# Padding rows scattered by index, a sum by matmul, and 48 steps of attention moved from the ordering of the entries to the experts

## The chip, the cores and the metric

The kernel runs on one core of one Trainium2 chip. The metric is device time in microseconds, as the median of several runs. One execution of it was taken by the hardware profiler; its trace gives the start and duration of every instruction. The engines are called as the profile calls them: PE (TensorE matmuls) and PEld (its weight loads), DVE (VectorE), ACT (ScalarE), POOL (GpSimd) and SP (SyncE, which here only issues DMAs). Each engine works through its own queue in order.

## The reference, cut to what matters

For x of 8 batches of 1024 rows of 256 numbers the kernel computes x + s * g.

```
xn = layernorm(x)
# attention over the 4 heads of each row, not over rows
q, k, v = (xn @ W + b).reshape(b, s, 4, 256)      for Wq, Wk, Wv
scores  = (q*cos . k*cos + q*sin . k*sin) / 16     # 4 x 4 for each row
s = softmax(scores) @ v, heads to rows (swapaxes), @ Wo + bo
# mixture of 8 experts, each row takes the best 2
gates = sinkhorn(xn @ router_w.T + router_b, 3 rounds)   # sums over experts, then over rows
top 2 gates of each row, normalised to sum 1
expert_out = sum over the 2: gate * ((relu(xn @ wg) * (xn @ wp)) @ wo)
g = silu(xn + expert_out)
out = x + s * g
```

## The kernel before, in words

The 8192 rows are 64 tiles of 128 rows, in 16 blocks of four. The work runs in five stages; two of them share TensorE with attention.

**Preparation.** `prepare` (L371 to L424) normalises a block, stores it row by row in `xn_d` (L422, in HBM) and turned in `xT_d` (L418). `xn_d`, and the result of the experts `z_d`, have 256 rows more than there are tokens: padding rows, where padded entries may point. After the last store GpSimd issues two plain DMAs: zeros into the padding rows of `xn_d` (L1032) and a padding list over all of `list_d` (L1035, 9088 KB).

**Routing and ordering.** `route` (L454) runs the gates, with one maximum and three sums over partitions on GpSimd (`partition_all_reduce`, L494 and L505). `order` (L540) finds for each of the 16384 entries (a row and its gate) its place in a list sorted by expert; it sums counts over partitions once more on GpSimd (L579). Beside both, `setup_values` prepares weights.

**Scattering the entries.** `scatter` (L635) writes the entries into `list_d` by index: 16 groups of 8 indirect DMAs, each of one column of 128 entries. The places of a group are cast to integers on VectorE (`place`, L639), and that cast is held behind `newest["dot"]`, the newest dot product that attention has issued when the group is written down. So the groups are spread over attention's steps: the first group comes ahead, then 32 steps, then each group followed by 15 steps, then 13. Ahead of it SP copies all of `xn_d` into `z_d` (L1060): the experts add their results to it.

**Attention** is a generator (`attention`, L819), which issues one small step at each call. A tile's scores (`score`, L653) are 9 steps: four chunks of matmuls into `py` (L662) that ScalarE copies to `qk` (L669), one step of four dot products on VectorE (`junk`, L675), and four in which the keys are weighted (`kx`, L700) and dotted. So a tile has 16 dots. `soften` (L713) is two steps for each block. `value` (L726) of a tile comes a block later, between the scores: two halves of matmuls `pu` (L745) with `u` (L752), then the mix of the heads. Ahead of the experts the mix is four matmuls with a `mixer` (L777), 3 steps in all; beside the experts, VectorE weights `u` itself (16 instructions, L764 and L768) and the matmul is a narrow one (L772), 4 steps in all. So a block is 50 steps ahead of the experts and 54 beside them, and the first block, which has no older values, 38. 32 + 15 times 15 + 13 = 270 steps are issued before the experts.

**Experts.** The list is cut in 71 tiles of 256 entries, each of one expert; 68 always run. For each, `fetch_expert` reads the entries (L840), casts the rows (L850), gathers them from `xn_d` (`xg`, L853, indirect), and loads three weight matrices (L864). `expert` turns the rows on TensorE (`ptr_g`, L878), multiplies (`pg`, `pp`, L890; ScalarE and VectorE between), and `down` (`po`, L906) scales by the gate and adds into `z_d` by index (L919). After each of the 408 steps of the experts one step of attention is issued, after every fourth two: 510 steps. The last three tiles run only if needed (L1075).

**Tail.** For each block, `fetch_last` (L947) loads z, x and s on SP, `finish` (L962) computes silu(z) * s + x and stores it (L967, GpSimd). Six steps of attention stand ahead of each, until attention is done; a block's result needs attention's result of its whole batch.

The order on each engine is that of the compiled program: the framework's scheduler takes instructions in nearly the order of the source and moves some ahead by estimated times. Names with a number in the program (`py_0_2881`) are one tile's buffers.

Of the kernel before, what the change touches and what calls it, by code (L numbers as in the profile page):

```python
# [9 lines left out]
F32 = mybir.dt.float32  # L10
# [6 lines left out]
P = 128  # L17
# [13 lines left out]
def recurrent_kernel(  # L31
# [20 lines left out]
    nc = tc.nc  # L52
    B, S, D = x.shape
    H = phase.shape[0]
    E, _, FF = ffn_g.shape
# [3 lines left out]
    R = HD // D  # L59
# [8 lines left out]
    M = G // P  # L68
# [35 lines left out]
    n = 1  # L104
# [349 lines left out]
    def route(pool, hot, entries):  # L454
# [22 lines left out]
        def flat(a):  # L477
            return a.rearrange("p b e -> p (b e)")
# [20 lines left out]
        for turn in range(SINKHORN_ITERS):  # L499
            if turn:  # L500
                nc.vector.tensor_reduce(rs, share, AX.X, ALU.add)
                nc.vector.reciprocal(rs, rs)
                nc.vector.tensor_tensor(share, share, per_tile(rs), ALU.mult)
            nc.vector.tensor_reduce(cm, by_expert(share), AX.X, ALU.add)
            nc.gpsimd.partition_all_reduce(flat(cs), flat(cm), P, bass_isa.ReduceOp.add)  # L505
            yield
            nc.vector.reciprocal(cs, cs)
            nc.vector.tensor_tensor(by_batch(share), by_batch(share), per_expert(cs), ALU.mult)
            yield
# [30 lines left out]
    def order(pool, hot, keep, placed):  # L540
# [35 lines left out]
        for i in range(R):  # L576
            rows = slice(i * J, (i + 1) * J)
            nc.vector.tensor_copy(quarter[rows, i], count[rows, :E])
        nc.gpsimd.partition_all_reduce(  # L579
            sums.rearrange("p i e -> p (i e)"),  # L580
            quarter.rearrange("p i e -> p (i e)"),
            P,
            bass_isa.ReduceOp.add,
        )
        total, prior = pool.tile([P, E], F32, name="o_total"), pool.tile([P, E], F32, name="o_prior")
        nc.vector.tensor_reduce(total, sums.rearrange("p i e -> p e i"), AX.X, ALU.add)
        nc.vector.tensor_tensor(
# [382 lines left out]
    def run(gen, n=None):  # L970
        done = 0
        while (n is None or done < n) and next(gen, StopIteration) is not StopIteration:
            done += 1
# [2 lines left out]
    xT_tiles, newest, attended, stored, beside_experts = {}, {}, set(), [], [False]  # L976
    x_rows, out_rows = (a.rearrange("b s d -> (b s) d") for a in (x, out))
    att_gen = attention()
    blank = const.tile([P, M * D], F32, name="blank")
    nc.vector.memset(blank, 0.0)  # L980
    empty = const.tile([P, M, LE], F32, name="empty")
    nc.vector.memset(empty, 0.0)
    for m in range(M):
        nc.vector.tensor_scalar(
            empty[:, m, :1], partition[:, :1], float(M), float(B * S + m), ALU.mult, ALU.add
        )

    ids = const.tile([P, T], F32, name="ids")
    nc.vector.tensor_copy(ids[:, :TB], column[:, :TB])
    n = TB  # L990
# [19 lines left out]
    with tc.tile_pool(name="prep", bufs=2) as prep:  # L1010
        with tc.tile_pool(name="setup", bufs=1) as setup:
            small_rows = fetch_setup(setup)
            for blk in range(7):
                fetch_rows(blk, prep, "x", 7)

            for blk, tag in ((7, "kx"), (8, "kx"), (9, "s_out"), (10, "s_out")):
                fetch_rows(blk, att, tag, 2)
            fetch_rows(11, att, "w", 1)
            bvT = setup_scores(setup, *small_rows)
            prepare(0, prep)  # L1020
        with tc.tile_pool(name="tail", bufs=1) as tail:
            for blk in range(12, T // TB):
                fetch_rows(blk, tail, f"x{blk}", 1)
            for blk in range(1, 4):
                prepare(blk, prep)
            linear(0, prep)
            for blk in range(4, T // TB):
                prepare(blk, prep)
                if blk % 4 == 3:
                    linear(blk - 3, prep)  # L1030
        with tc.issue_after(stored[-1].ins):
            nc.gpsimd.dma_start(  # L1032
                xn_d[B * S :].rearrange("(p m) d -> p (m d)", m=M), blank
            )
            nc.gpsimd.dma_start(  # L1035
                list_d.rearrange("(n p m) c -> p n (m c)", p=P, m=M),
                empty.rearrange("p m c -> p (m c)").unsqueeze(1).to_broadcast([P, N, M * LE]),
            )
    with tc.tile_pool(name="routing", bufs=1) as routing:
        hot = routing.tile([P, E, K, T], F32, name="hot")  # L1040
        entries = routing.tile([P, K * T * 2 + LE], F32, name="entries")
        nc.vector.memset(entries, 0.0)
        for n in range(K):
            nc.vector.tensor_copy(pairs_of(entries)[:, n, :, 0], ids)

        keep = routing.tile([P, E, K * T], F32, name="keep")
        nc.vector.memset(keep, 1.0)
        nc.vector.memset(keep[:, :, :1], 0.0)

        values = setup_values(bvT)  # L1050
        for n, _ in enumerate(route(routing, hot, entries)):
            if n > 2:
                run(values, 1)
        placed = []
        run(order(routing, hot, keep, placed))
        run(values)
        put = scatter(entries, placed[0])
        next(put)

        nc.sync.dma_start(z_d, xn_d)  # L1060
        run(att_gen, 32)
        for _ in put:
            run(att_gen, 15)
        run(att_gen, 13)
    before_experts = newest["score"]
    fin = ctx.enter_context(tc.tile_pool(name="fin", bufs=2))
# [2 lines left out]
    ffn = middle.enter_context(tc.tile_pool(name="ffn", bufs=2))  # L1069
    beside_experts[0] = True  # L1070
    for n, _ in enumerate(experts(0, SURE)):
        run(att_gen, 1 if n % 4 else 2)

    held = nc.values_load(first_spare[:1, :1], min_val=0, max_val=E)
    with tc.If(held < E):  # L1075
# [47 lines left out]
```

## Time and profile before

| what | value |
|---|---|
| median of 14 runs | 1714.77 us (1711.72 to 1716.53) |
| the profiled execution: its own time | 1714.96 us |
| its span, first to last instruction | 1713.2 us |
| mean granted TensorE clock | 0.976 |
| busy: PE, DVE, ACT, POOL | 1623.8, 1205.4, 432.5, 674.7 us |
| HBM read, written | 178.17, 76.41 MB |
| first matmul of an expert (`pg`) | 410.25 us |
| last matmul of the 68th expert (`po`) ends about | 1587.3 us |
| dots of a tile of the first block | about 10 us |
| a tile of attention ahead of the experts | about 12 us |

A line of a timeline has the start in us, the duration in us (of several instructions of one kind in a row, if there is an x and a number), the engine, the line of the kernel, the operation, what it writes and reads, the shapes, and in brackets how long the engine stood idle before it and what released it. A line of busy time by stages has the stretch, its length, and for PE, PEld, DVE, ACT and POOL the busy us and the number of instructions; then the granted clock of TensorE, the mean busy share of the 16 DMA engines and GB/s. A matmul in 32-bit floats leaves two records in the trace: eight matmuls of a tile's scores are 16 records of L662. Ends of matmuls are modelled, so records in a row overlap a little; what a run of them takes is read from the chain of waits, where only the time to the next is counted.

### The profile page before, as it was taken

How to read it: one execution, taken by the hardware profiler on the slowest of the kernel's cores; microseconds unless marked ns; L12 is line 12 of the kernel's file. 1: busy time of each engine (PE TensorE's matmuls, PEld its weight loads, DVE VectorE, ACT ScalarE, POOL GpSimd, SP SyncE). 2: the span in 40 equal slices, each digit the busy share in tenths (PEclk: the TensorE clock that was granted, in tenths of full speed). 3: DMA queues.
4: the chain of work that ended last, by engine and by line, in shares of the span. 5: the costliest groups of instructions: out<-in, count | busy, mean ns of one | idle time of the engine just before them, and what ended most of it. 6: DMA issues, size and time to landing. Idle time of an engine off the chain costs nothing.

```text
span 1713.2 us, 22964 instructions
## 1 busy us (share of the span) xinstructions
PE 1623.8 (95%) x7695; PEld 1002.8 (59%) x7695; DVE 1205.4 (70%) x3717; ACT 432.5 (25%) x816; POOL 674.7 (39%) x593
## 2 busy tenths in 40 slices
PE   6897799999999999999999999999999999999773
PEld 5373344445666666766666666666666666666331
DVE  6669999998575575765765756656657567476694
ACT  3742222222222212222222222222222222222322
POOL 0315876575243433343343434344423443331111
PEclk8898999999999999999999999999999999999887
DMA  8992022125544554544544544544545545542688
GB/s 271 360 358 89 31 73 62 58 66 199 148 120 127 141 130 114 149 119 111 164 119 113 147 124 119 152 115 132 145 111 141 140 117 129 141 109 52 214 262 305
DMA packets 149305, 247.48 MB, mean 144 GB/s; under 512 B 15304, under 2 KB 93168, under 8 KB 149008
## 3 DMA queue, kind: packets, MB, share of 16 engines
q1 hardware_dynamic: 105904, 164.42, 29.2%
q0 software_dynamic: 41264, 77.37, 19.6%
q10 hardware_dynamic: 2016, 4.20, 0.7%
q8 instruction: 62, 1.02, 0.2%
q14 instruction: 59, 0.48, 0.1%
HBM read 178.17 MB, written 76.41 MB: 149 GB/s over the span
## 4 chain that ended last, share of the span: by engine, by line
PE 78%; DVE 12%; DMA 6%; issue 2%; POOL 1%; ACT 1%; SPq 0%; POOLq 0%; ACTq 0%; DVEq 0%
PE py L662 18%; PE pg L890 14%; PE po L906 14%; PE pp L890 14%; PE pu L745 10%; DVE junk L675 5%; DVE kx L700 3%; PE ptr_g L878 2%; PE po_s L772 1%; DMA fz<-z_d 1%; PE ptr_x L410 1%; PE po_s L777 1%; DMA fs<-s_d 1%; DMA out_dram<-fz 1%; DMA z_d<-y,row 1%
## 5 line engine op out<-in xcount | busy, mean ns | idle before, releaser
L662 PE MATMUL py<-w_qk,xTa 128*128 128x512 f32 x1024 | 476.8, 601 | 27.0 <-ACT qk L669 27.0
L919 POOL DMA_INDIRECT z_d<-y,row x136 | 234.6, 1725 | 566.0 <-ACT y L916 473.1
L675 DVE CUSTOM_DVE_ANT_0 junk<-qk,kx,lg 128x256 f32<-128x256 f32 x768 | 323.6, 477 | 0.1
L662 PEld LDWEIGHTS py<-w_qk,xTa 128*128 128x128 f32 x1024 | 189.8, 191 | 222.1 <-issue 182.2
L675 DVE CUSTOM_DVE_ANT_0 junk<-qk,lg 128x256 f32<-128x256 f32 x256 | 113.2, 479 | 265.1 <-ACT qk L669 264.9
L669 ACT COPY qk<-py 128x512 f32<-128x512 f32 x256 | 149.6, 586 | 464.6 <-PE py L662 426.3
L890 PE MATMUL pg<-xgT,wg 128*128 128x256 f32 x1088 | 266.0, 386 | 0.3
L890 PE MATMUL pp<-xgT,wp 128*128 128x256 f32 x1088 | 259.0, 380 | 0.0
L906 PE MATMUL po<-wd,hid 128*128 128x256 f32 x1088 | 257.1, 382 | 0.0
L890 PEld LDWEIGHTS pg<-xgT,wg 128*128 128x128 f32 x1088 | 200.9, 190 | 89.2 <-issue 37.0
L745 PE MATMUL pu<-w_vo,xTa 128*32 128x512 f32 x2048 | 248.0, 597 | 0.3 <-PEq L1075 0.3
L906 PEld LDWEIGHTS po<-wd,hid 128*128 128x128 f32 x1088 | 203.3, 190 | 66.9 <-issue 43.3
L700 DVE TENSOR_TENSOR kx<-qk,mixrow 128x1024 f32<-128x1024 f32 (+1 forms) x256 | 233.5, 949 | 0.1
L890 PEld LDWEIGHTS pp<-xgT,wp 128*128 128x128 f32 x1088 | 205.5, 190 | 32.3 <-issue 3.3
L642 POOL DMA_INDIRECT list_d<-entries,place x128 | 179.7, 1404 | 76.0 <-DVE place L639 40.6
L899 DVE TENSOR_TENSOR hid<-pp,hid 128x512 f32<-128x512 f32 x136 | 93.3, 686 | 145.5 <-PE pp L890 145.5
L764 DVE SCALAR_TENSOR_TENSOR w<-u,sc,w 128x256 f32<-128x256 f32 x456 | 192.3, 477 | 0.9
L853 POOL DMA_INDIRECT xg<-xn_d,row x136 | 160.4, 1179 | 51.1 <-issue 47.8
L898 ACT ACTIVATE hid<-pg 128x512 f32<-128x512 f32 x136 | 81.2, 597 | 301.6 <-PE pg L890 286.8
L745 PEld LDWEIGHTS pu<-w_vo,xTa 128*32 128x32 f32 x2048 | 57.1, 109 | 132.1 <-issue 121.9
L916 ACT ACTIVATE y<-po,entry 128x256 f32<-128x256 f32 x136 | 57.1, 471 | 231.9 <-PE po L906 231.9
L752 DVE TENSOR_TENSOR u<-pu,b_vo 128x512 f32<-128x512 f32 x128 | 85.9, 682 | 17.7 <-PE pu L745 17.1
(208 smaller groups left out, 985.6 us busy)
## 6 DMA issues: line engine op xcount, KB each, us to landing
wg<-in_L_ffn_wg_dram SPq DMA_DIRECT2D x68, 512.0 KB, 3.8
wp<-in_L_ffn_wp_dram SPq DMA_DIRECT2D x68, 512.0 KB, 4.4
wd<-in_L_ffn_wo_dram SPq DMA_DIRECT2D x68, 512.0 KB, 3.9
list_d<-empty POOLq DMA_DIRECT2D x1, 9088.0 KB, 56.0
z_d<-xn_d SPq DMA_DIRECT2D x1, 8448.0 KB
x<-in_L_attn_x_dram SPq DMA_DIRECT2D x16, 512.0 KB, 8.4
xn_d<-x POOLq DMA_DIRECT2D x16, 512.0 KB, 5.7
s_d<-s_out SPq DMA_DIRECT2D x64, 128.0 KB, 3.3
```

The costliest lines, as they stand in the source:

```text
L642: put = nc.gpsimd.indirect_dma_start(list_d, bass.IndirectOffsetOnAxis(ap=piece[:, c : c + 1], axis=0), entries[:, at * 2 : at * 2 + LE], ...
L662: newest["score"] = nc.tensor.matmul(py, xT[:, t, k], w[:, k, cols], start=(k == 0), stop=(k == KD - 1),)
L669: nc.scalar.copy(flat[:, cols], py)
L675: newest["dot"] = nc.vector.tensor_tensor_reduce(junk, qk[:, 0, h], k, 1.0 / math.sqrt(D), lg[:, tile_no, E + at : E + at + 1], ALU.mult, ...
L700: nc.vector.tensor_tensor(kx[:, :w], k, mixrow[:, at : at + w].unsqueeze(2).to_broadcast([P, w, 2, D]), ALU.mult,)
L745: nc.tensor.matmul(pu[i * J : (i + 1) * J, :], xT[:, t, k, i * J : (i + 1) * J], w_vo[:, k, i, cols], start=(k == 0), stop=(k == KD - 1),)
L764: nc.vector.scalar_tensor_tensor(w[:, h], part, share, w[:, h], ALU.mult, ALU.add)
L853: nc.gpsimd.indirect_dma_start(xg[:, m], None, xn_d, bass.IndirectOffsetOnAxis(ap=row[:, m : m + 1], axis=0),)
L890: nc.tensor.matmul(dst[:, f], w[:, k, at : at + P], xgT[:, k], start=(k == 0), stop=(k == KD - 1),)
L899: nc.vector.tensor_tensor(h, pp, h, ALU.mult)
L906: nc.tensor.matmul(po[:, m], hid[:, f, m * P : (m + 1) * P], wd[:, f], start=(f == 0), stop=(f == KF - 1),)
L919: nc.gpsimd.indirect_dma_start(z_d, bass.IndirectOffsetOnAxis(ap=row[:, m : m + 1], axis=0), y[:, m], None, compute_op=ALU.add,)
```

## The change

The source is changed at five places. Line numbers in the text are those of the kernel before; behind the edits they are larger by 2 to 17.

- The padding rows of `xn_d` are no longer written by a plain DMA after the preparation. Two indirect DMAs on GpSimd, with the row numbers in a new tile `padding`, scatter a zero tile there, held behind the last sum over partitions of `route` (`newest["columns"]`). The zero tile `blank` is half as wide.
- `z_d` gets the rows of `xn_d` without the padding (still on SP, written down earlier in the source), and its padding rows from the zero tile by a DMA of their own. The scattered padding and this copy are declared not to depend on each other.
- The sum over partitions in `order` is a matmul of a 128 x 128 tile of ones with the counts, into PSUM, and a copy by VectorE, and no longer an operation of GpSimd.
- Ahead of the experts: 14 steps after the first group and 13 after each other one, and 13 at the end: 222 steps, and not 270.
- Beside the experts: two steps of attention after two of every five steps of the experts, and not after one of four: 572 steps, and not 510.

```diff
@@ route
-            nc.gpsimd.partition_all_reduce(flat(cs), flat(cm), P, bass_isa.ReduceOp.add)
+            newest["columns"] = nc.gpsimd.partition_all_reduce(
+                flat(cs), flat(cm), P, bass_isa.ReduceOp.add
+            )
@@ order
-        nc.gpsimd.partition_all_reduce(
-            sums.rearrange("p i e -> p (i e)"),
-            quarter.rearrange("p i e -> p (i e)"),
-            P,
-            bass_isa.ReduceOp.add,
-        )
+
+        pq = ps_gp.tile([P, R * E], F32, tag="gp", name="pq")
+        nc.tensor.matmul(
+            pq, ones, quarter.rearrange("p i e -> p (i e)"), start=True, stop=True
+        )
+        nc.vector.tensor_copy(sums.rearrange("p i e -> p (i e)"), pq)
@@ main part
-    blank = const.tile([P, M * D], F32, name="blank")
+    blank = const.tile([P, D], F32, name="blank")
...
+    padding = const.tile([P, M], mybir.dt.int32, name="padding")
+    nc.vector.tensor_copy(padding, empty[:, :, 0])
...
         with tc.issue_after(stored[-1].ins):
             nc.gpsimd.dma_start(
-                xn_d[B * S :].rearrange("(p m) d -> p (m d)", m=M), blank
-            )
-            nc.gpsimd.dma_start(
                 list_d.rearrange("(n p m) c -> p n (m c)", p=P, m=M),
...
+    copied = nc.sync.dma_start(z_d[: B * S], xn_d[: B * S])
+    tc.add_to_no_dep_group("padding", copied.ins)
+    nc.sync.dma_start(
+        z_d[B * S :].rearrange("(p m) d -> p m d", m=M),
+        blank.unsqueeze(1).to_broadcast([P, M, D]),
+    )
...
+        with tc.issue_after(newest["columns"].ins):
+            for m in range(M):
+                pad = nc.gpsimd.indirect_dma_start(
+                    xn_d,
+                    bass.IndirectOffsetOnAxis(ap=padding[:, m : m + 1], axis=0),
+                    blank,
+                    None,
+                )
+                tc.declare_no_dep(pad.ins, group="padding", reason="rows behind those copied")
+                tc.add_to_no_dep_group("padding", pad.ins)
         placed = []
         run(order(routing, hot, keep, placed))
         run(values)
         put = scatter(entries, placed[0])
         next(put)
-
-        nc.sync.dma_start(z_d, xn_d)
-        run(att_gen, 32)
+        run(att_gen, 14)
         for _ in put:
-            run(att_gen, 15)
+            run(att_gen, 13)
         run(att_gen, 13)
...
     for n, _ in enumerate(experts(0, SURE)):
-        run(att_gen, 1 if n % 4 else 2)
+        run(att_gen, 2 if n % 5 < 2 else 1)
```

## The prediction

> **What bounds the kernel now.** I read the busy tenths, then the busy time by stages, then the queues of TensorE, GpSimd and VectorE where the experts begin, then the tail.
>
> ```profile
> PE   6897799999999999999999999999999999999773
> ```
>
> One digit is 42.8 us. TensorE is full but for the ends and slices 4 and 5 (128 to 214 us). By stages (PE, PEld, DVE, ACT, POOL busy, granted clock, DMA share, GB/s):
>
> ```profile
> 197.00:280.00 83.00, 82.65 (x382) 35.26 (x381) 83.00 (x282) 17.54 (x33) 60.48 (x55) 1.00 0.20 63
> 600.00:1000.00 400.00, 399.88 (x1917) 266.48 (x1916) 255.84 (x757) 94.09 (x183) 155.70 (x139) 1.00 0.50 129
> ```
>
> From 197 us up to the experts TensorE and VectorE are both full; beside the experts TensorE alone is (399.88 of 400), VectorE at 64%. A step of attention moved from the first stage to the second is therefore not hidden: it is paid in TensorE time in both. What counts is the idle time of TensorE, and that sits where the experts begin. GpSimd's queue:
>
> ```profile
> 147.25 30.18 POOL L642 DMA_INDIRECT list_d<-entries,place  x1 [11.47 <-DVE place L639]
> 177.74 8.44 POOL L642 DMA_INDIRECT list_d<-entries,place  x1 [0.30 <-issue]
> ...
> 380.26 0.97 POOL L642 DMA_INDIRECT list_d<-entries,place  x1 [0.39 <-DVE place L639]
> ...
> 393.26 3.67 POOL L840 DMA_DIRECT2D entry<-list_d  x5 [1.84 <-DMA list_d<-entries,place]
> 398.84 0.19 POOL L850 CAST row<-entry 128x2 int32<-128x2 f32 x1 [1.91 <-DMA entry<-list_d]
> ```
>
> The first two scatters take 38.6 us, so that the third starts at 186.48; all later ones take 0.97 to 2.0. The last group of eight starts when its cast is done (VectorE, 379.83), and then a fixed chain runs: eight scatters to 391.4, their landing, the read of the list to 398.8, the gather, landed at 407.9. That is 28.1 us from cast to the first expert's transposes. TensorE's queue:
>
> ```profile
> 155.65 9.59 PE L662 MATMUL py<-w_qk,xTa 128*128 128x512 f32 x16 [9.24 <-ACT qk L669]
> 175.60 7.13 PE L662 MATMUL py<-w_qk,xTa 128*128 128x512 f32 x16 [2.85 <-ACT qk L669]
> ...
> 342.94 1.99 PE L777 MATMUL po_s<-u,mixer 128*128 128x256 f32 x8
> 344.86 3.64 PE L745 MATMUL pu<-w_vo,xTa 128*32 128x512 f32 x32
> 348.43 6.28 PE L662 MATMUL py<-w_qk,xTa 128*128 128x512 f32 x14
> 354.54 1.89 PE L777 MATMUL po_s<-u,mixer 128*128 128x256 f32 x8
> 356.27 1.02 PE L662 MATMUL py<-w_qk,xTa 128*128 128x512 f32 x2
> 357.22 3.64 PE L745 MATMUL pu<-w_vo,xTa 128*32 128x512 f32 x32
> ...
> 407.92 0.55 PE L878 MATMUL ptr_g<-ident,xg 128*128 128x128 f32 x3 [0.61 <-DMA xg<-xn_d,row]
> ```
>
> The chain is just covered now: TensorE waits 0.61 us for the gather at 407.9.
>
> **The change, part by part.** Sums are made against the profiled execution: span 1713.2 us, 1714.96 with what lies around it; that is 0.2 above the median, 1714.77.
>
> *Padding rows.* A plain DMA of 256 KB (0.55 us of GpSimd) goes; two indirect scatters come, held on GpSimd behind the last column sum, which ends at 118.55. GpSimd is idle from there to 135, and to 147 but for the 0.60 us of the sum that the change takes away. What the 38.6 us are, no view says (the DMA engines moved 1 GB/s meanwhile); the rows show only that the first indirect DMA of the program pays them. If the pads take them, they end at 157.2, and the groups can start then instead of the third scatter's 186.5. With nothing to take it would be 121; with the memory traffic (98% until 140) in the way it is later. None of this is on the path: in backlog GpSimd needs 1.41 us a scatter (54 from 186.48 to 262.82), 11.3 a group, so fifteen groups from 157.2 end at 326.9, ahead of the last cast (342.6, below); pads may end as late as 173. I take 0, and the case that they take nothing is a rival.
> [...]
>
> *Copies to z_d.* The copy of 8.4 MB waits for the stores of xn_d alone (it was issued at 90.28; at most a microsecond earlier now); 256 KB from a zero tile go ahead of it on SP's queue, which held nothing else until 225. Both end about 250 us before the first add into z_d. 0.
>
> *The sum in the ordering.* A partition sum (0.60, and 0.43 that VectorE waits) becomes one matmul and a copy of some 0.2: 0 within 0.3. But in the compiled order the matmul stands behind the first two of four chunks of tile 0's scores. These end at 128.9, the operand is ready at 135.1: TensorE stalls 6.2 us. Queued behind it are chunks 3 and 4, for which VectorE's first dot (138.56) waits. Cover: TensorE has 9.24 idle at 146 anyway, and chunk 3 would be copied by 137.8. Not covered is a slow start: 16 records took 9.59 after 9.24 us of idle, 7.13 after 2.85. For 6.2 that is between 0 and 2.46 on TensorE, 0 to 1.7 on the first dot. I take 1.0.
>
> *Fewer steps ahead of the experts.* In the compiled order TensorE loses, ahead of the first expert's transposes, 64 records of L662, 112 of L745, 32 of L777. Runs in the chain of waits give 0.429 (8 in 3.43), 0.1116 (32 in 3.57), 0.249 (8 in 1.99): 27.5 + 12.5 + 8.0 = **48.0 us** that could be had. But the chain must be covered too. The last cast now stands two dots before the end of tile 16; in the trace of before that place is 341.3 (tile 16's dots end at 342.1). With 1.0 from above and 0.3 for the copy and three more casts: 342.6. The chain of 28.1 gives 370.7. TensorE's order behind that place is as in the rows above: po_s, pu, 14 of py, po_s, 2 of py and half a pu, which end at 359.1, so 360.4 here: **it stalls 10.3 us** where it stalled 0.6. By the code 26 steps follow the last group where 28 did. But its cast waits for the newest dot issued, and before that was tile 19's last, with tile 20's chunk steps already issued and all its dots to come; now it stands inside tile 16's dots. In TensorE's work the cover falls from 27.2 us (379.83 to 407.04) to 17.8 (342.6 to 360.4). The first transposes move from 407.9 to 370.7: **-37.2**.
> After such a stall TensorE is slow again: 2.46 (155.65 against 175.60); take **+2.3**, between 0 and 2.5.
> [...]
>
> *More steps beside the experts.* 62 more steps; in the compiled order TensorE gets 72 more records of L662, 144 of L745 and 32 of L772 (0.57 for 8): 30.9 + 16.1 + 2.3 = **+49.3**. The number of changes between kinds of matmul stays (731 and 730). VectorE gets 4.5 tiles at some 18 us (16 dots at 0.41, kx 3.6, u 1.3, 16 weightings at 0.42) on 1230, so 64% becomes 69%: covered, and without that cover it would cost nothing until it is above TensorE.
> The last expert's matmuls, 1587.3 now, end 14.4 later.
>
> *The tail* (1587.3 to 1713.2; same columns):
>
> ```profile
> 1611.00:1627.00 16.00, 16.00 (x58) 6.37 (x57) 16.00 (x44) 6.48 (x10) 1.66 (x2) 0.88 1.04 396
> 1627.00:1643.00 16.00, 15.45 (x63) 6.32 (x61) 16.00 (x43) 5.16 (x8) 1.51 (x2) 1.00 0.81 276
> 1643.00:1662.00 19.00, 8.43 (x46) 4.00 (x44) 19.00 (x48) 3.70 (x5) 1.96 (x3) 0.74 0.78 246
> ```
>
> VectorE is full to 1662: results leave in pairs, with the dots of one tile between two pairs (stores at 1613.2, 1629.3, 1646.2, 1661.6: a period of 16.3). The changed order has two tiles between the pairs in place of three; the other is done while the last adds land (to 1603.9), when VectorE had little to do. But the bytes stay: 19.5 MB move from 1643 to 1708.5, at 298 GB/s. What is late next is DMA. At the same rate nothing is gained; at 357 (1682 to 1696) 10.9; a whole period would be 16.3. At 330, between the 325 and the 357 of the last stretches, it is 6.4: **-6**.
>
> Sum: -37.2 + 2.3 + 49.3 - 6 = +8.4, so 1723.4: **1723 us**.
>
> **Rivals.**
> 1. *No stall at the entry; faster.* If the chain from last cast to gather takes no more than the 17.8 us of work in front of it, 9.7 and 2.3 go: 1711.4, and lower with a better tail. For it: the kernel before was covered. Against it: every link (11.2, 1.8, 5.6, 9) is a row with nothing of attention in it. It decides at a chain of some 22 (6 less, and no slow start), where the time is that of before; faster by more than can be told from none is below 18.6.
> 2. *The tail gives a whole period*, 11 to 16: 1713 to 1718. For it: VectorE is full for 51 us. Against: DMA is at 94% and 99% of its share from 1662 to 1696.
> 3. *The tail gives nothing*: 1729.
> 4. *The pads don't do what they are for*: the first list scatter takes the 38.6 again. Then 126 scatters at 1.41 from 186.5 end at 364.2 instead of 354.2, +10: 1733. For it: no row shows two such scatters to different tensors in turn. Against: the gather at 400, another kind again, took 1.04.
>
> **How the numbers follow.** Forecast 0.57, no stall 0.12, whole period 0.14, empty tail 0.08, pads useless 0.06, other 0.03. The range, 1711 to 1731, leaves out the last two and half of the second, 0.15; in it lie the bounds of the slow starts and of the tail. A difference under 0.2% (3.4 us) can't be told from none: slower takes nearly all of the forecast, the empty tail and the useless pads, 0.69; same the whole period and the edges, 0.20; faster the first rival, 0.11.
>
> **What would show it.** GpSimd: a long indirect DMA at 119, none at 147. TensorE: some 10 us before the first transposes on the gather, these near 371, and a slow run behind it; the last expert matmul near 1602. Tail: results in pairs, closer after the third. Transposes near 360 prove me wrong at the entry; a last expert matmul more than 3 us off with the right entry, in the price of a step; a tail other than 120 us, in the DMA.

## The result

The changed kernel takes **1734.74 us** (median of 6 runs, 1733.79 to 1735.81), the kernel before 1714.64 (median of 28, 1709.97 to 1718.37). The ratio is 1.0119, with a 95% interval from 1.0109 to 1.0129. The forecast was 1723, its range ended at 1731: the direction was right, but the kernel became 20.1 us slower, and not 8.4. The profiled execution took 1734.44, its span is 1732.7.

The tables below cut the span at two places that every trace shows: the start of the first transposes of an expert (`ptr_g`), and the start of the last matmul of the 68th expert (`po`). The expert stage lies between the two.

| us | before | after | difference | forecast |
|---|---|---|---|---|
| first transposes | 407.0 | 368.0 | -39.1 | -37.2 |
| expert stage | 1181.6 | 1246.1 | +64.5 | +51.6 (49.3 + 2.3) |
| tail | 124.5 | 118.6 | -5.9 | -6 |
| span | 1713.2 | 1732.7 | +19.5 | +8.4 |

The forecast's -37.2 runs from 407.92 to 370.7, the transposes that wait for the second gather; after, these stand at 369.94, which is -38.0. The first transposes need the first gather only, so in this table the wait between the two gathers (0.61 us before, 1.53 after) lies in the expert stage.

Two of the three terms came out within 2 us. GpSimd's queue after (start, duration, engine, line, operation; in brackets the idle time before it):

```profile
116.93 1.07 POOL L1065 DMA_INDIRECT xn_d<-blank,padding  x1 [0.18 <-issue]
118.30 0.99 POOL L1065 DMA_INDIRECT xn_d<-blank,padding  x1 [0.30 <-issue]
146.51 0.97 POOL L644 DMA_INDIRECT list_d<-entries,place  x1 [27.22 <-DVE place L641]
...
353.49 1.24 POOL L644 DMA_INDIRECT list_d<-entries,place  x1 [0.31 <-issue]
356.28 3.67 POOL L842 DMA_DIRECT2D entry<-list_d  x5 [1.56 <-DMA list_d<-entries,place]
360.36 0.48 POOL L852 CAST row<-entry 128x2 int32<-128x2 f32 x1 [0.41 <-DMA entry<-list_d]
```

The padding took 1.07 and 0.99 us, and so did the first list scatter, 0.97, where it took 30.18. The 38.6 us were not taken over: they are gone. The last cast starts at 343.28 (forecast 342.6), and the chain behind it has the links foreseen: 26.7 us to the second gather's transposes, where 28.1 was taken. TensorE's queue after:

```profile
133.32 0.63 PE L583 MATMUL pq<-o_quarter,ones 128*128 128x32 f32 x2 [6.00 <-DVE o_quarter L580]
...
359.18 1.92 PE L747 MATMUL pu<-w_vo,xTa 128*32 128x512 f32 x16
367.96 0.45 PE L880 MATMUL ptr_g<-ident,xg 128*128 128x128 f32 x1 [6.85 <-DMA xg<-xn_d,row]
369.94 0.90 PE L880 MATMUL ptr_g<-ident,xg 128*128 128x128 f32 x3 [1.53 <-DMA xg<-xn_d,row]
370.64 1.91 PE L664 MATMUL py<-w_qk,xTa 128*128 128x512 f32 x2
372.48 3.47 PE L747 MATMUL pu<-w_vo,xTa 128*32 128x512 f32 x16
```

The stall ahead of the sum is 6.00 (forecast 6.2). The work ahead of the experts ends at 361.1, and TensorE then waits 6.85 and 1.53 us for the gather, 8.4 in all (forecast 10.3). Behind it the slow start: 16 records of `pu` last 1.92 us ahead of the wait (second row) and 3.47 behind it (last row). The granted clock was 0.50 there (busy PE, PEld, DVE, ACT and POOL, granted clock, DMA share, GB/s):

```profile
365.40:375.60 10.20, 6.11 (x22) 1.82 (x22) 4.36 (x17) 0.58 (x1) 6.66 (x9) 0.50 1.06 362
```

At a clock of 1.00 those 6.11 us of TensorE would be half as long, an estimate from the 0.50; so the slow start cost about 3.1. The stage itself, and the tail, in the same columns:

```profile
600.00:1000.00 400.00, 399.38 (x1905) 258.22 (x1903) 272.80 (x813) 91.92 (x180) 151.44 (x132) 1.00 0.47 124
```

```profile
1680.00:1733.00 53.00, 21.66 (x128) 8.63 (x126) 27.07 (x28) 10.65 (x13) 6.78 (x9) 0.75 0.89 331
```

TensorE is as full beside the experts as it was (399.38 of 400), VectorE at 68%, and the granted clock is 1.00. So nearly all of the 12.9 us that the forecast lacks in the stage is TensorE's own time; the waits in the stage are the 1.53 us between the gathers and 1.1 us, in four waits, of the narrow `po_s` for VectorE's weighting. In the last 53 us 331 GB/s are moved (298 before), where 330 was taken for the tail.

**Where they come from.** Counted from one record's start to the next, by kind of matmul, in the stage: `py` +32.3 us for 72 records (0.449 each; 0.429 was forecast), `pu` **+23.8 for 144 (0.165 each; 0.112 was forecast)**, narrow `po_s` +1.7, one `mixer` matmul left over from the stage before +1.7, `pg` and `pp` +2.6, `ptr_g` +2.0, `po` +0.4. The slow start is spread over `py`, `pu` and `ptr_g`. The oddity is `pu`. Before, a half is issued whole or as 8 and 8 records; after, some stand as here:

```profile
628.58 1.06 PE L745 MATMUL pu<-w_vo,xTa 128*32 128x512 f32 x8
637.97 1.92 PE L745 MATMUL pu<-w_vo,xTa 128*32 128x512 f32 x16
```

```profile
659.08 1.05 PE L747 MATMUL pu<-w_vo,xTa 128*32 128x512 f32 x2
...
665.43 1.06 PE L747 MATMUL pu<-w_vo,xTa 128*32 128x512 f32 x8
...
668.35 1.06 PE L747 MATMUL pu<-w_vo,xTa 128*32 128x512 f32 x6
```

The first two rows are of before. In the other three, of after, one half of `pu`, 16 records, is issued in three pieces, with matmuls of the expert between. Two records take as long as eight. Counted from a piece's first record to the start of whatever comes next, 16 records last 1.85 us in every case but the one behind the stall, 8 about 1.05, and a lone matmul (2 records) 0.98. In the trace before no `pu` is a lone matmul; after there are seven, by the order that the scheduler chose. That gave a theory: **four matmuls of 32 columns, to four column groups, run side by side in the time of one; whoever cuts such a group pays it twice.**

### The profile page after: what moved, and what is told of

The parts are those of the page before. It is cut to its first block, busy times and chain, and to the rows that moved or that the text cites. A ratio compares the mean times of both kernels' runs of the same rounds, so it can differ in the third digit from the quotient of the medians.

```text
span 1732.7 us, 23018 instructions
## 1 busy us (share of the span) xinstructions
PE 1632.7 (94%) x7697; PEld 1002.0 (58%) x7697; DVE 1228.4 (71%) x3779; ACT 432.0 (25%) x816; POOL 651.8 (38%) x593
## 3 DMA queue, kind: packets, MB, share of 16 engines
q8 instruction: 62, 1.02, 0.2%
## 4 chain that ended last, share of the span: by engine, by line
PE 75%; DVE 16%; DMA 3%; issue 3%; ACT 1%; POOL 1%; SPq 0%; POOLq 0%; ACTq 0%; DVEq 0%
PE py L664 20%; PE po L908 13%; PE pg L892 12%; PE pp L892 12%; PE pu L747 10%; DVE junk L677 6%; DVE kx L702 3%; DVE w L766 2%; PE ptr_g L880 2%; PE po_s L774 1%; PE po_s L779 1%; PE ptr_x L410 1%; DVE u L754 1%; PE pw L327 1%; DMA fs<-s_d 1%
## 5 line engine op out<-in xcount | busy, mean ns | idle before, releaser
L921 POOL DMA_INDIRECT z_d<-y,row x136 | 239.3, 1760 | 622.7 <-ACT y L918 533.7
L747 PE MATMUL pu<-w_vo,xTa 128*32 128x512 f32 x2048 | 256.5, 601 | 0.1
L766 DVE SCALAR_TENSOR_TENSOR w<-u,sc,w 128x256 f32<-128x256 f32 x504 | 211.8, 476 | 1.0
L855 POOL DMA_INDIRECT xg<-xn_d,row x136 | 161.9, 1191 | 59.2 <-issue 38.6
L644 POOL DMA_INDIRECT list_d<-entries,place x128 | 145.8, 1139 | 89.6 <-DVE place L641 53.9
```

The lines of the kernel that those rows point to most:

```text
L644: put = nc.gpsimd.indirect_dma_start(list_d, bass.IndirectOffsetOnAxis(ap=piece[:, c : c + 1], axis=0), entries[:, at * 2 : at * 2 + LE], ...
L747: nc.tensor.matmul(pu[i * J : (i + 1) * J, :], xT[:, t, k, i * J : (i + 1) * J], w_vo[:, k, i, cols], start=(k == 0), stop=(k == KD - 1),)
L766: nc.vector.scalar_tensor_tensor(w[:, h], part, share, w[:, h], ALU.mult, ALU.add)
L855: nc.gpsimd.indirect_dma_start(xg[:, m], None, xn_d, bass.IndirectOffsetOnAxis(ap=row[:, m : m + 1], axis=0),)
L921: nc.gpsimd.indirect_dma_start(z_d, bass.IndirectOffsetOnAxis(ap=row[:, m : m + 1], axis=0), y[:, m], None, compute_op=ALU.add,)
```

## The experiments

The times are medians, or one execution where one is given; the kernel before was timed again along with each group of runs and stands at 1714.8 to 1715.2, but for one group, which is told. "Lone" counts the lone `pu` matmuls of the stage in the trace.

| run | steps ahead, beside | first transposes | expert stage | tail | lone | us |
|---|---|---|---|---|---|---|
| before | 270, 510 | 407.0 | 1181.6 | 124.5 | 0 | 1714.6 |
| after | 222, 572 | 368.0 | 1246.1 | 118.6 | 7 | 1734.7 |
| old steps | 270, 510 | 409.0 | 1181.4 | 124.2 | 0 | 1716.4 |
| steps alone | 222, 572 | 377.1 | 1245.5 | 118.4 | 7 | 1742.3 |
| covered | 222, 572 | 360.8 | 1241.5 | 118.6 | 7 | 1723.9 |
| tail | 222, 510 | 368.0 | 1187.2 | 168.3 | 0 | 1727.5 |
| bunched | 222, 574 | 363.1 | 1237.6 | 112.0 | 1 | 1714.6 |
| whole quads | 222, 572 | 361.1 | 1233.8 | 117.1 | 2 | 1715.2 |
| whole, fewer | 222, 558 | 362.5 | 1219.3 | 127.4 | 0 | 1711.1 |
| cut groups | 222, 558 | 363.1 | 1240.5 | 124.3 | 17 | 1730.1 |
| one after other | 270, 510 | 406.3 | 1206.6 | 124.1 | 2 | 1738.8 |

### Is it the steps or the other edits?

The changed kernel with the old counts:

```diff
-        run(att_gen, 14)
+        run(att_gen, 32)
         for _ in put:
-            run(att_gen, 13)
+            run(att_gen, 15)
...
-        run(att_gen, 2 if n % 5 < 2 else 1)
+        run(att_gen, 1 if n % 4 else 2)
```

> The changed kernel with the step counts of before on both sides of the experts' begin (32, 15 and 13 ahead; one step beside, two after every fourth). What is left of the change: the padding rows by indirect DMA, the sum by matmul, the split copy. Theory A (these parts are worth nothing, the step counts are all of the loss): 1714.6 to 1716.0, that is the kernel before plus at most the 1.3 us of the 6.0 us stall ahead of the matmul sum; first transposes of an expert at 408 to 409, expert stage 1181 us as before, no indirect DMA of 30 us on GpSimd. Rival (the parts cost something of the 20 us themselves): above 1718.

Measured: 1716.43, ratio 1.0006 (0.9997 to 1.0016), 0.4 above the range of theory A and below the rival. Padding, sum and copies are worth nothing that can be told; the loss comes with the step counts.

The kernel before with the new counts alone (the same lines the other way):

> The kernel before with the step counts of the change alone (14, 13, 13 ahead; two steps after two of five beside). Theory A (the 38.6 us of the first two list scatters are put on the path once the groups are pressed together): third scatter at 186 again, last scatter ends at about 364 where the changed kernel ends at 354.7, first transposes at about 379, stall before them 17 to 19 us; total about 9 us above the changed kernel, 1742 to 1745. Rival (GpSimd makes it up, or the long scatters don't come): first transposes at 369 to 371, total 1732 to 1735. In both, the expert stage is 1244 us, as in the changed kernel, if it is a matter of the steps alone.

Measured: 1742.31, ratio 1.0152 (1.0135 to 1.0169). The third scatter takes 9.72 and the fourth starts at 185.98; the last ends at 362.0, the first transposes come at 377.1, and TensorE waits 17.4 us for the gathers (17 to 19 was expected). So the other edits are worth 9 us at the entry and 7.6 in the medians once the groups are pressed together (forecast, as a rival: 10), and the stage is the same 1245.5: its length belongs to the steps.

### What the stall costs

The changed kernel with the 222 steps put otherwise:

```diff
         for _ in put:
-            run(att_gen, 13)
-        run(att_gen, 13)
+            run(att_gen, 12)
+        run(att_gen, 28)
```

> The changed kernel with the same 222 steps ahead of the experts, but 12 and not 13 behind each group, and 28 and not 13 behind the last: the chain from the last cast to the first transposes starts some 12 us earlier and TensorE has as much work to put in front. Theory A (the stall of 8.4 us and the slow start of some 2.9 behind it are lost outright): the last cast at about 331, first transposes at 360 with under 1 us of waiting, no slow run behind, expert stage and tail unchanged; 1723 to 1725. Rival (VectorE or GpSimd is what is late there, so that the time comes back as other waits): 1730 or more.

Measured: 1723.91, ratio 1.0050 (1.0033 to 1.0066). TensorE at the entry:

```profile
358.97 1.92 PE L747 MATMUL pu<-w_vo,xTa 128*32 128x512 f32 x16
360.82 0.66 PE L880 MATMUL ptr_g<-ident,xg 128*128 128x128 f32 x4
361.32 1.02 PE L664 MATMUL py<-w_qk,xTa 128*128 128x512 f32 x2
362.27 1.92 PE L747 MATMUL pu<-w_vo,xTa 128*32 128x512 f32 x16
```

No bracket with a wait ahead of the transposes, and the next `pu` takes its usual 1.92. The entry is 7.1 us earlier, the stage 4.6 shorter: 1.5 are the second wait, 3.1 the slow start (the granted clock is 1.00 from 358 to 368 us here). As far as the stall goes the theory holds: 10.8 of the 20 us. It also says what the steps cost without a stall: 1241.5 - 1181.6 = 59.9 for 62, where 49.3 was forecast.

### What a step costs beside the experts and in the tail

The changed kernel with the 510 steps of before beside the experts:

> The changed kernel with 222 steps ahead of the experts, but beside them 510 as before: 62 steps more are left to the tail than in the changed kernel, 48 more than before. Theory A (a step beside the experts costs about 1.0 us of TensorE): the expert stage falls from 1244.5 to 1181 to 1185 us, last matmul of an expert at about 1552. The tail is the open part: at the 0.43 us a step that the change gave back there (6.0 us for 14 steps) it is 118.3 + 27 = 145 us and the total 1699; if VectorE, which is full for 50 us there, has to pay its whole 1.4 us a step (18 us of VectorE to a tile of 12.5 steps), it is 118.3 + 87 = 205 and the total 1759. Rival to the first part (the extra time of the expert stage is no price of steps but belongs to the early begin): expert stage above 1195.

Measured: 1727.46, ratio 1.0068 (1.0051 to 1.0085). The stage is 1187.2 (1181 to 1185 was expected; the second wait and the slow start are still in it), so the steps beside are paid one by one. The tail, 168.3, is 49.7 longer than after for 62 steps: neither of the two prices but between. The first 14 steps taken out of the tail of before were worth 0.4 us each; 48 more put into it cost 0.9 each.

### Cut groups, number of changes, or only the number of steps

Three patterns of steps beside the experts, from the covered kernel:

```diff
-        run(att_gen, 2 if n % 5 < 2 else 1)
+        run(att_gen, 7 if n % 5 == 0 else 0)
```

> The run with the covered chain (12 steps behind each group, 28 at the end), but with attention beside the experts in bunches: seven steps after every fifth step of the experts, 574 in all instead of 572 (8 matmuls more of the scores, 6.9 us, fall before the last expert). In the compiled order the changes between kinds of matmul fall from 576 to 486, the runs of narrow matmuls from 87 to 61, and the tiles of pu whose group of four side by side is cut from 11 to 1. Theory B (the 10 us that the forecast missed are narrow groups cut in two, at 0.93 us each, and some 0.1 us for each run end): expert stage 1241.5 + 6.9 - 14 = 1234, total 1716. Theory C (a step beside the experts costs 0.97 us wherever it stands): stage 1243 to 1249, total 1725 or more. Against both: bunches may leave TensorE waiting for VectorE or ScalarE between them, then above 1730.

Measured: 1714.64, ratio 0.9996 (0.9987 to 1.0006). Stage 1237.6, with `py` 9.0 longer for its 16 records more and `pu` 8.2 shorter. That lies between theory B (1234) and theory C (1243 and more), nearer to B; the time is below both also because the tail is 6.6 us shorter.

```diff
+        run(att_gen, (2,2,0,2,2,0)[n % 6] + (n % 15 == 2))
```

> The run with the covered chain, with the same 572 steps beside the experts put differently: 2, 2, 0, 2, 2, 0 after the six steps of an expert, and one more after every fifteenth. The numbers of matmuls of each kind stay as they are; in the compiled order 2 groups of four narrow matmuls are cut instead of 11, runs of narrow matmuls fall from 87 to 72, changes of kind from 576 to 555. Theory B (cut groups, 0.93 us each, and run ends): 8.4 for the cut groups and 3.2 for the rest, stage 1241.5 - 11.6 = 1230, total 1712 to 1713. Theory C (a step costs 0.97 us wherever it stands): 1724.

Measured: 1715.22, ratio 1.0001 (0.9991 to 1.0010): 8.7 us gone with the same work in another order; the stage is 7.7 shorter, of the 11.6 expected. The count that the expectation goes by was of pieces in the compiled order, and too high: a half in pieces of 2, 8 and 6 records counts twice there but costs about one piece more. The trace has 7 lone matmuls in the one and 2 in the other, `pu` is 5.8 us shorter.

That still fits a price for each change of kind. These two patterns of 558 steps don't:

```diff
+        run(att_gen, (2,2,0,2,2,0)[n % 6] + (n % 30 == 2))    # whole, fewer
+        run(att_gen, (0,0,4,0,0,4)[n % 6] + (n % 30 == 2))    # cut groups
```

> The covered chain (222 steps ahead, 12 behind each group, 28 at the end), and beside the experts 558 steps: 2, 2, 0, 2, 2, 0 after an expert's six steps and one more after every thirtieth. So the 48 steps fewer ahead come back one for one, and the tail is left with as many as in the kernel before. In the compiled order no group of four narrow matmuls is cut; 66 runs of narrow matmuls, 535 changes of kind. Prices from the runs so far (2 records of the scores 0.858 us, a half of pu 1.85, a cut 0.93): the stage falls by 14 to 24 us from the 1233.8 of the run with the 572 steps in the same pattern, to 1216 to 1220; first transposes at 361, tail 124 us as before. Total 1703 to 1706 and faster than both kernels. Rival (a step moved costs 0.97 us wherever it stands, and its cuts nothing): stage 1228, total 1714 to 1716.

> The same 558 steps in another pattern: 0, 0, 4, 0, 0, 4 after an expert's six steps, one more after every thirtieth. Numbers of matmuls of each kind as in the other run of this call with 558 steps; but in the compiled order 23 groups of four narrow matmuls are cut in two (none there), 83 runs of narrow matmuls (66), and only 483 changes of kind (535). Theory B (cut groups): 23 times 0.93 and some run ends, 24 us above the other, 1727 to 1731. Theory C (it is the number of changes of kind): below the other by 5 to 10. Theory D (only the number of steps counts): equal within 3 us.

Measured: 1711.11, ratio 0.9981 (0.9972 to 0.9990), and 1730.09, ratio 1.0089 (1.0075 to 1.0104). The second has 52 changes of kind **fewer** (18, if `pg` and `pp` count as two kinds), and its stage is 21.2 us longer. `pu` makes 16.5 of them, and it has 17 lone matmuls at 0.98: 16.7. The other 4.7 are small differences of all the other kinds. The number of changes falls as an explanation, and so does a flat price of a step. The first beats both kernels, though by less than expected (1703 to 1706): stage 1219.3 as foreseen, but first transposes 1.5 later and a tail of 127.4 in place of 124, for a reason that no run shows. Run again beside the version with casts (below) it was 1712.95, ratio 0.9984 (0.9975 to 0.9993):

> The kernel with 558 steps beside the experts and no cut group, as before: 0.2% below the kernel before (0.9981 with an interval from 0.9972 to 0.9990), 1711 us if that is at 1715.

### Side by side, or one after the other

The kernel before, loops exchanged:

```diff
-            for k in range(KD):
-                for i in range(R):
+            for i in range(R):
+                for k in range(KD):
                     nc.tensor.matmul(
                         pu[i * J : (i + 1) * J, :],
```

> The kernel before with the two inner loops of pu exchanged: the two matmuls that add into the same 32 columns now follow each other, and a group of four neighbours goes no longer to four different column groups. Number, shape and place of all matmuls stay as they are. Theory B (four narrow matmuls on different column groups run side by side in the time of one, 0.9 us): the eight of a half take 4.5 us (if every second one still runs beside its neighbour) to 7.8 us (if none does) where they took 1.85; with 76 halves beside the experts that alone is 200 to 450 us. Rival (a narrow matmul is simply cheap, 0.22 us each, and the extra cost is that of a change of kind): 1.85 us a half again and 1713 to 1720 in all.

Measured: 1738.78 in one execution. Neither theory had this. `pu` in its stage:

```profile
631.75 1.90 PE L745 MATMUL pu<-w_vo,xTa 128*32 128x512 f32 x4
637.24 1.93 PE L745 MATMUL pu<-w_vo,xTa 128*32 128x512 f32 x12
641.02 1.04 PE L745 MATMUL pu<-w_vo,xTa 128*32 128x512 f32 x2
643.92 1.94 PE L745 MATMUL pu<-w_vo,xTa 128*32 128x512 f32 x14
```

A whole half is still 1.87 us, so the four need not be neighbours in the queue: theory B was too strict there. But the scheduler now cuts 15 halves, 13 of them behind two matmuls of one column group, and those four records take 1.83 alone, the other twelve 1.86. `pu` in the stage is 24.1 us longer (166.2 for 142.1), with the same matmuls in the same number: 13 x 1.83 and 2 x 0.98 are 25.8, less some 3 that the kernel before pays for halves issued as 8 and 8 (1.05 twice, for 1.85); whole halves at 1.87 for 1.85 add one more. The count of pieces is nearly the same as before (78 for 76), so a fixed price of a piece, or of a change from wide to narrow matmuls, can't explain it. The rule that fits all pieces in both orders is: **a piece lasts as long as its fullest column group, 0.9 us for each matmul in it** (1, 2, 3 and 4 matmuls in it: 0.98, 1.85, 2.71 and 3.57 us). What is shown is that a cut costs this much; that the groups run at the same time inside the array is how I read it.

### What became of the 38.6 us

The kernel before with the matmul sum alone; and the old steps with GpSimd's sum put back:

> The kernel before with the matmul sum of the ordering alone; padding rows by the plain DMA. For the 38.6 us of the first list scatters. Theory D (they come after the sum over partitions on GpSimd at 135 us, whatever is scattered first): first scatter at 147 takes 1 to 2 us. Theory E (the plain DMA of the padding rows is what holds them): 30 us again, the third scatter at 186. The time is 1714 to 1717 in both.

> The changed kernel with the step counts of before and with the sum over partitions in the ordering back on GpSimd; the padding rows stay indirect. Theory D (the sum on GpSimd is the cause): the first list scatter at 147 is long again and the third starts at about 186. Theory E (the plain DMA is the cause): the first list scatter takes 1 to 2 us. Theory F (the first indirect DMA pays and the pads have taken it while nobody waited): also 1 to 2 us, so that this run and the one with the matmul alone must be read together: only if both are short is it neither alone. The time is 1713 to 1717 in all.

Measured, in one execution each: 1719.33 (1714 to 1717 was expected) with the first list scatter at 1.08 us, and 1713.31 with it at 30.11. GpSimd of the second:

```profile
117.78 1.08 POOL L1065 DMA_INDIRECT xn_d<-blank,padding  x1 [0.17 <-issue]
...
134.24 0.59 POOL L581 PARTITION_ALL_REDUCE o_sums<-o_quarter  x1 [14.09 <-DVE o_quarter L580]
146.28 30.11 POOL L644 DMA_INDIRECT list_d<-entries,place  x1 [11.45 <-DVE place L641]
```

The padding doesn't take anything over; the sum brings the 30 us back (theory D). Its first transposes stand at 406.9, those of the old steps at 409.0: the matmul sum costs 2.1 us at the entry, where 1.3 was forecast. That suggested a version with all four chunks of the first tile ahead of the sum:

```diff
+        run(att_gen, 4)
         run(order(routing, hot, keep, placed))
...
-        run(att_gen, 14)
+        run(att_gen, 10)
```

> The run with 558 steps and no cut group, with four of the first 14 steps issued ahead of the ordering: all four chunks of the first tile's scores then stand ahead of the matmul sum on TensorE, and not two, so that the 6.0 us stall in front of it holds up nothing that VectorE needs next. By the two runs that differ only in the sum (first transposes 408.96 with the matmul, 406.9 with the partition sum): first transposes 1.5 to 2.5 us earlier than in the other run of this call, total 1 to 2.5 us less. Rival (TensorE's lost 6 us count in full, wherever they stand, since it is busy up to the experts): no difference.

Measured: median 1730.21, ratio 1.0059 (1.0028 to 1.0090). Its executions fall in two groups, two at 1707.75 and 1709.03, as expected, ten from 1727.40 to 1735.43; the profile is of the second group. There GpSimd's first two scatters take 22.58 and 10.55 us, up to 186.6, though there is no sum on GpSimd in the ordering. It is then behind until its last scatter ends at 367.2, and the first transposes come at 380.4, 18 us late. So theory D is not the whole cause. Over all profiles: with that sum on GpSimd a scatter is held in five of five, with the matmul in one of thirteen.

In these four profiles with long scatters (before, steps alone, sum put back, chunks first) each of them ends 0.9 to 1.0 us after VectorE issues something that is neither a dot nor a weighting of keys. So 20 small casts were put among the dots of the kernel before:

```diff
...
+                with tc.issue_after(newest["dot"].ins):
+                    ticks.append(nc.vector.tensor_copy(tick, ids[:, :1]))
...
```

> The kernel before, with nothing changed but this: on VectorE, 20 casts of one column (0.15 us each) stand among the dots of the first block, one behind each group of four. In four profiles with a long first list scatter (30.18, 10.20, 30.11 and 22.58 us) the scatter that is held ends 0.9 to 1.0 us after the next instruction of VectorE that is neither a dot nor a weighting of keys: a place cast or the reduction of the softening (cast at 176.41, end at 177.43; reduction at 185.24, end at 186.18). Theory P (while VectorE runs dots and keys without a break GpSimd can't finish it, and any small other instruction lets it through): the first scatter ends within 5 us and the 38.6 us become 10 at most; the third starts by 160 instead of 186. Theory Q (GpSimd is busy with something of its own for a fixed time, and the casts only happened to stand there): 30 and 8 us again, the third at 186. Time 1713 to 1718 in both: the groups are not on the path here.

Its GpSimd and its VectorE (the casts alone):

```profile
145.90 5.29 POOL L642 DMA_INDIRECT list_d<-entries,place  x1 [11.52 <-DVE place L639]
151.50 3.10 POOL L642 DMA_INDIRECT list_d<-entries,place  x1 [0.30 <-issue]
154.90 1.36 POOL L642 DMA_INDIRECT list_d<-entries,place  x1 [0.30 <-issue]
...
176.39 5.60 POOL L642 DMA_INDIRECT list_d<-entries,place  x1 [1.27 <-DVE place L639]
```

```profile
150.17 0.14 DVE L1047 CAST tick<-ids 128x1 int32<-128x1 f32 x1
...
153.66 0.14 DVE L1047 CAST tick<-ids 128x1 int32<-128x1 f32 x1
155.34 0.14 DVE L1047 CAST tick<-ids 128x1 int32<-128x1 f32 x1
```

The first three scatters end at 151.19, 154.60 and 156.26, that is 1.02, 0.94 and 0.92 us after a cast. So the holds end as theory P says, and theory Q's fixed time falls, in the one execution there is. But the casts shorten the holds and don't remove them: eight scatters up to 185.5 us still take 3.1 to 5.6 us, 33 in all, and each ends 0.9 to 1.0 us after a cast; ten scatters are done by 186 us, where the kernel before had done two. Not every cast frees a scatter: one at 146.75 in this run and one at 157.24 in the run with the chunks first passed without. In the run with the exchanged loops a scatter was held for 38.98 us, past a cast at 174.59, and ended 1.0 us after the reduction of the softening. (The one execution took 1722.14; the kernel before was at 1739.44 in this group of runs, so the time says nothing.)

Does that make the version with the chunks first sound?

> The run with the chunks first, with the same 20 casts among the dots of the first block. That run was spread from 1707.75 to 1735.43, and in the profile (1731.6) the first two list scatters take 33 us and the first transposes come at 380.4 instead of 362.5. Theory P: the scatters take 1 to 5 us in every execution, the spread goes, first transposes at 360 to 362, total 1707 to 1711 (its two short executions were 1707.75 and 1709.03). Theory Q: spread as before, most executions at 1727 to 1735.

> The kernel with 558 steps, no cut group, four chunks first and the 20 casts among the dots once more, beside the kernel with the 558 steps alone. In the call before, the kernel before itself took 1739 us instead of 1715, so the two can't be set against each other over the two calls. If the scatters are no longer held, the first transposes stand about 2 us earlier than without chunks first: 1 to 3 us below the other run of this call, with a spread of no more than 10 us, and 0.25 to 0.45% below the kernel before if that is at 1715. Rival: GpSimd is held in some executions all the same, spread over 20 us, median above the other run.

Measured: 1725.56 beside a kernel before at 1739.44, ratio 0.9929 (0.9906 to 0.9952), in that group of runs; then 1714.40, ratio 1.0018 (0.9995 to 1.0040). In both profiles the scatters are short (0.97 and 0.96 us first). But the second time five of twelve executions still took 1723 to 1728, the others 1710 to 1715. The rival is right, on the spread and on the median (1712.95 for the other run), and the first transposes came only 0.7 us earlier (362.6 for 363.4). The two profiles are of the same kernel, 1726.67 and 1710.57 us, and where they differ is the entry: first transposes at 377.5 and 362.6, with the same stage (1219.2) and nearly the same tail (128.2 and 127.0). Up to 197 us they run alike; then, in the longer one, TensorE stands still for 5.01 us before 223.64 and 2.92 before 303.63, and the granted clock is 0.50 behind each (8 records of `py` take 5.38 us behind the second and 3.70 ahead of it). So a held scatter is not the only thing that delays the entry; what it is there stays open.

## Why the prediction was wrong

**The step that failed** is "More steps beside the experts ... +49.3". The counts were right (72 and 144 records, and of the 32 narrow ones 24 in the stage and 8 behind it), and the number of changes of kind did stay (729 and 730 in the stage). The price of `pu`, 0.1116 a record, was read from runs of 32 records ahead of the experts, where nothing stands between. I looked at how often the kind changes and not where: in the new order seven halves are cut inside a group. Without any stall the term is 59.9: `py` 31.4 (30.9 forecast), `pu` 22.3 (16.1), narrow `po_s` 1.7 (2.3), and unforeseen the left-over mixer, 1.7, and `pg`, `pp`, 2.6, of which 2.1 are in the records just ahead of a narrow run, which take 0.309 or more instead of 0.216. So `pu` makes 6.2 of the 10.6 us by which the term was too small. That its size was about right for uncut groups, the run with 558 steps and no lone matmul shows: it pays 1219.3 - 1181.4 = 37.9 for 48 steps, **0.79 each**; the forecast had 49.3 / 62 = 0.80. The sum agrees better than its parts (`pu` took 10.4 where its price gives 12.5, `py` 25.7 for 24.0), so some of that is luck. With seven cuts it is 0.97.

**Slow start:** forecast 2.3, measured 3.1. The wait of 1.5 us in front of its second half is not a miss: the forecast's stall of 10.3 ran to the second gather, and the two waits together are 8.4. The measured 3.1 is above the 2.5 that I had taken as the upper end. The clock of 0.50 lasted 10.2 us, from 365.4 to 375.6, with the second wait inside it.

**Entry:** -38.0 for -37.2, between the transposes that the forecast meant (its 407.9; the very first stand at 407.04, and at 367.96 after, the -39.1 of the table). The last cast came 0.7 us later than forecast, the chain behind it was 1.4 shorter. The point "its cast waits for the newest dot issued" and the cover of 17.8 us against a chain of 28.1 were right, and the covered run shows that the stall was avoidable with the same number of steps. The end of the chain, and not the end of TensorE's work in front of it, set the entry.

**Tail:** -5.9 for -6. The number was chosen between 0 and 16 by the rate of the DMA. The rate came out over the last 53 us (331 for 330 GB/s); over the last 65, about the stretch that the forecast had reckoned with, it is 307. So part of the hit is luck, and no run tests why the tail is shorter. (The last `po` of before starts at 1588.64, and not ahead of the 1587.3 that the tail was counted from.)

**Pads:** "If the pads take them, they end at 157.2" did not come true: the first indirect DMA of the program doesn't pay for the others, it took 1.07 us. That was without cost, since the groups were early enough either way. The rival "the pads don't do what they are for" was at 1733, next to the measured time, for a reason that didn't happen: GpSimd was not late. A right number is no proof of its mechanism; the first transposes at 368 are.

**Sum:** of the 11.1 us between forecast (+8.4) and span (+19.5), counted by the table, 10.6 are the price of the steps and 2.3 the second wait and slow start, less 1.9 at the entry.

## What to carry to other kernels

A price per record holds only for the surroundings that it was read from (`pu`: 0.112 us ahead of the experts, 0.165 for the records added beside them): where narrow matmuls go to several column groups, count in the compiled order how many groups are cut, and not how often the kind of work changes. Before moving work from one full stage to another compare the price of a unit in each (here 1.00 us ahead, 0.79 to 0.97 beside, 0.4 to 0.9 in the tail): at its best, with no group cut and no stall, the move was worth 0.2%, and here the stall and the cuts were paid on top. Where a fixed chain must be covered, move work behind its start, not away.

## What the runs showed of the hardware

- A `pu` piece of 2, 6 or 8 records on different column groups takes 0.98, 0.99 and 1.05 us, one of 16, 24 or 32 takes 1.85, 2.71 and 3.57; 4 records on one column group 1.83.
- A record of `pp` or `po` just ahead of a run of narrow matmuls takes 0.309 us and not 0.216.
- While VectorE runs 128x256 dots and key weightings without a gap (busy for 40.00 of the 40 us from 146 to 186 in the kernel before), an indirect DMA on GpSimd can be held for 30.18 us (38.98 in one run). The holds end 0.9 to 1.0 us after a small cast or reduction on VectorE; why, no run here shows. In other profiles the same scatters pass in 0.97 us beside the same dots: what decides that is open.
- The first indirect DMA of the changed kernel started 0.18 us behind the operation ahead of it and took 1.07.
